# One queue in written order for the first cross attention, and a reordered step list in the last feed-forward block of a Perceiver kernel

## The chip, the core and the metric

The kernel is one program on one core of a Trainium2 chip. It is written in Tile: instructions are recorded tile by tile, the framework derives the semaphores, and outside of regions marked as manual a scheduler orders what each engine does. The metric is the device time of one execution in microseconds, as the median of the runs shown.

## The reference, cut to what matters

Twelve residual blocks follow each other on `x` of 2 x 256 tokens of 256 features (T = 512 columns, features on partitions), with a context of 2 x 4096 rows. Two of them are touched.

```python
# L0_xattn: 16 heads of 16, queries from layernorm(x), keys and values from the context
q = ln(x) @ Wq + bq;  k = ctx @ Wk + bk;  v = ctx @ Wv + bv
x = x + softmax(q k^T / 4 + mask) v
# L3_ffn: two layers of local attention (8 heads of 64, window 128, causal) and a gated MLP
q, k = l2norm(q) * qs, l2norm(k) * ks
q = q * cos * scale + rotate_half(q) * sin * scale        # k likewise, with 1 / scale
x = x + (softmax(8 q k^T + mask) v) @ wo
x = x + (a * gelu(g)) @ w2 + b2
```

All arithmetic is float32. The rest of the blocks, the key features of L3_xattn that are computed inside of L0_xattn among them, are not changed.

## The kernel before

**Cross attention.** `ContextAttention` works in 8 units, one per batch and group of four heads. A unit has 16 steps, and `attend` is a loop over all steps `g`. A step issues the first scores of its unit (`first_scores`, L1257: eight matmuls into four PSUM banks, whose maxima VectorE takes at L1265 and L1271), from step 18 on also the second scores of the unit before it (L1287), their exponentials on ScalarE (L1296) and the products with the values (L1308), and then the step's fills. A fill is a projection that a planner, `plan_with`, has placed by due times: a pair of key tiles (`project_keys`, L1167), half a value tile (`project_values`, L242 into `v_ps`) or key features for L3_xattn (`Focus.project`, L242 into `f_ps`). PE, VectorE and ScalarE follow the written order (`tc.manual_schedule`); GpSimd and SyncE, whose instructions are mostly DMA issues, are ordered by the scheduler.

**Keys.** A pair of key tiles needs two 512 KB loads of the context (`load_keys_ctx`, tiles `ctx_k`, one buffer each). In layer 0 the 2nd, 4th and 6th pair are loaded instead into six value tiles that are still free (`key_homes`, `xv` in the trace). After the matmuls ScalarE adds the bias (`k_dense`, L1177). Then `project_keys` issues the load for the next pair, two mask rows (L1185, 8 KB each) and eight copies of 16 rows (L1195, 32 KB each) that spread the dense keys to the head rows of `xa_k`. For the first six pairs the copies of the first tile go to ScalarE's DMA queue and those of the second to SyncE's; from the seventh on all go to SyncE's. Eight semaphores serve all of these DMAs in turn: the issue of a DMA waits until the DMA that used its semaphore last, eight earlier, has landed.

```python
queue = nc.scalar if self.spare and j < self.BY_ACT and i == 0 else nc.sync
for g in range(NG):
    at = i * HR + g * DH
    queue.dma_start(out=k[g * HP : g * HP + DH, :], in_=dense[at : at + DH, :])
```

**The last block.** `l3_ffn` makes queries and keys in four chunks of 128 features. `products` and `normalize` compute a chunk and its inverse norms (matmul with `same`, Ln and Exp on ScalarE at L2483 and L2484, the scaling on VectorE at L2485, four DMAs that swap halves), and `turn` applies the rotation (two multiplications at L2495 and L2496 for each of query and key, and a sum on GpSimd at L2497). `self_attention` then runs 16 items in pairs `m`. For each `m` it issues, in this order: `share` of the pair before (reciprocals on VectorE L460, the scaling of the probabilities on GpSimd L464), a hook `before`, the scores with their maxima (L419, L433) and exponentials (L445), a hook `along`, the weighing of the pair before that (L488, copied out by VectorE at L495), the transposes of the pair before (L475, copied out by VectorE at L480 and ScalarE at L478), and a hook `behind`, which `l3_ffn` does not use. Chunk 3 is normalized in `before(1)`, chunk 2 is turned in `along(1)`, chunk 3 in `along(3)` and `along(4)`.

Of the kernel before, what the change touches and what calls it, by code (L numbers as in the profile page):

```python
# [108 lines left out]
class Net:  # L109
# [51 lines left out]

    def load(self, *names, now=None):


        nc = self.nc
        t = self.weights.tile([P, 2048], F32, tag="w", name=f"w_{names[0]}")
        at, parts = 0, []
        for name in names:
            src = self.ins[name]
            n = int(np.prod(src.shape[1:]))  # L170
            letters = "abcde"[: len(src.shape) - 1]
            flat = src
            view = t[:, at : at + n]
            if len(letters) > 1:
                flat = src.rearrange(f"p {' '.join(letters)} -> p ({' '.join(letters)})")
                sizes = {c: s for c, s in zip(letters, src.shape[1:])}
                view = view.rearrange(f"p ({' '.join(letters)}) -> p {' '.join(letters)}", **sizes)
            issue = partial(nc.sync.dma_start, out=t[:, at : at + n], in_=flat)
            if now is None or len(parts) < now:
                issue()  # L180
            else:
                self.postponed.append(issue)
            parts.append(view)
            at += n
        assert at <= 2048, (names, at)
        return parts[0] if len(parts) == 1 else parts
# [331 lines left out]
    def context_attention(self, x, q_bias, k_bias, v_bias, wq, wk, values, layer, alive=None, block=None):  # L518

        tc = self.tc
        by_program = {mybir.EngineType.PE, mybir.EngineType.DVE, mybir.EngineType.Activation}  # L530
        to_values = lambda: tc.tile_pool(name="xa_v", bufs=1, reuse_waits="tile")
        with (
            tc.tile_pool(name="xa", bufs=1, reuse_waits="tile") as big,
            tc.tile_pool(name="xa_ctx", bufs=2, reuse_waits="tile") as cpool,
            to_values() if layer == 0 else nullcontext() as vpool,
        ):
            a = ContextAttention(self, layer, big, cpool, vpool, (wk, k_bias), v_bias)
            if layer == 0:
                for issue in self.postponed:
                    issue()  # L540
                a.load_keys_ctx()
                self.nc.sync.dma_start(out=self.vectors, in_=self.ins["vectors"])
                self.focus = Focus(self)
            a.wv, wo = values()
            if block is not None:
                with tc.manual_schedule(engines={mybir.EngineType.PE}), self.stage():
                    x = block(x, a.begin(3))
            with tc.manual_schedule(engines=by_program):
                return self.attend_to_context(a, x, q_bias, wq, wo, alive, nullcontext(vpool) if vpool else to_values())

    def attend_to_context(self, a, x, q_bias, wq, wo, alive, values):
        tc = self.tc
        with self.stage():
            norm = self.center(self.halves(x), load=a.layer > 0)
            if a.layer == 0:
                self.context_constants()
            if not a.begun:
                a.beginning = a.begin(2)
                run(a.beginning, 1)
            a.take_queries(norm, wq, q_bias, alive)  # L560
        with (
            self.banks(mm=4, sc=2, acc=0),
            values as vpool,
            tc.tile_pool(name="xa_p", bufs=1, reuse_waits="tile") as ppool,
            tc.tile_pool(name="focus", bufs=2, reuse_waits="tile") as fpool,
        ):
            return a.attend(vpool, ppool, fpool, x, wo)
# [237 lines left out]
class ContextAttention:  # L805
# [9 lines left out]
    VALUE_TILES = 11  # L815
    BY_ACT = 6
    SPARE = 3

    def __init__(self, net, layer, big, cpool, vpool, keys, v_bias):
        self.net, self.nc, self.layer, self.cpool = net, net.nc, layer, cpool  # L820
# [12 lines left out]
        if layer > 0:  # L833
            self.joined = Joined(net, big, lambda b, c: self.q[b * NC16 + c])
        self.spare = vpool is not None
        self.key_homes = {}
        if self.spare:
            self.vpool = vpool
            for n in range(self.SPARE):
                self.key_homes[2 * n + 1] = [self.new_values() for _ in range(2)]  # L840
        self.begun, self.beginning = 0, iter(())
# [248 lines left out]
    def attend(self, vpool, ppool, fpool, x, wo):  # L1090
# [4 lines left out]
        if self.layer == 0:  # L1095
            nc.gpsimd.memset(self.new[P // 2 :, ND - 1, S:], 0.0)
        for _ in range(4):
            self.load_values_ctx()
        focus.start(self.layer, fpool)
        fills = self.plan()  # L1100
        n = len(self.UNITS)

        rankings = {}
        for g in range((n + 1) * PER + LAG + 2):
            second = g - PER - LAG
            if 0 <= second < n * PER:
                self.scores(second // PER, second % PER)
            if g < n * PER:
                pair = self.first_scores(g // PER, g % PER)
            run(self.beginning)  # L1110
            if 1 <= g < n:
# [8 lines left out]
            for fill in fills.get(g, ()):  # L1120
                fill()
            for kc in self.rankings.get(g, ()):
                if kc not in rankings:
                    y, _, factor = focus.chunks[kc]
                    rankings[kc] = focus.sparsify(fpool, y, factor)
                run(rankings[kc], 1)
# [6 lines left out]
            for kc in self.weighings.get(g, ()):  # L1133
                run(focus.weighing[kc], 1)
        return self.new


    def load_keys_ctx(self):
        b, kc = next(self.key_loads, (None, None))
        if b is None:  # L1140
            return
        pair, homes = [], self.key_homes.pop(len(self.key_ctx), None)
        for i in range(2):
            if homes:
                flat = homes[i].rearrange("p k v -> p (k v)")[:, : ND * KC]
                ctx = flat.rearrange("p (d n) -> p d n", d=ND)
            else:
                ctx = self.cpool.tile([P, ND, KC], F32, name=f"ctx_k{i}", tag=f"ctx_k{i}", bufs=1)
            self.nc.sync.dma_start(out=ctx, in_=self.net.ins["ctxT"][b, kc + i])
            pair.append(ctx)  # L1150
        self.key_ctx.append(pair)

    def project_keys(self, j, first, n=1):
# [26 lines left out]
        tiles = [self.key_tiles[(2 * j + i) % self.KEY_TILES] for i in range(2)]  # L1180

        def write_mask(i):
            rows = tiles[i].rearrange("(g r) n -> g r n", r=HP)
            mask = net.key_masks[self.layer, b * NKC + kc + i]
            nc.sync.dma_start(out=rows[:, DH + 1], in_=mask.unsqueeze(0).to_broadcast([NG, KC]))  # L1185

        if not self.spare or j != 2 * self.SPARE - 1:
            self.load_keys_ctx()
        for i, k in enumerate(tiles):
            if j > 0:  # L1190
                write_mask(i)
            queue = nc.scalar if self.spare and j < self.BY_ACT and i == 0 else nc.sync
            for g in range(NG):
                at = i * HR + g * DH
                queue.dma_start(out=k[g * HP : g * HP + DH, :], in_=dense[at : at + DH, :])  # L1195
        if j == 0:
            for i in range(2):
                write_mask(i)

    def new_values(self):  # L1200
        return self.vpool.tile([P, KC // P, VW], F32, name="xv", tag="xv", bufs=self.VALUE_TILES)

# [9 lines left out]
    def project_values(self, b, kc, k2, first, n=1):  # L1212

        net, nc = self.net, self.nc
        if k2 == first == 0:
            v = self.new_values()
            nc.gpsimd.memset(v, 1.0)
            self.values[b, kc] = v
# [116 lines left out]
def l0_attn(net, x):  # L1335
    nc, tc = net.nc, net.tc
    wdq, wdkv, wuv = net.load("L0a_wdq", "L0a_wdkv", "L0a_wuv")
    wups = net.load("L0a_wuq", "L0a_wuk")
# [1065 lines left out]
def l3_ffn(net, x):  # L2404
# [8 lines left out]
    with tc.tile_pool(name="l3f", bufs=1, reuse_waits="tile") as big, tc.tile_pool(name="l3f_w", bufs=2, reuse_waits="tile") as work:  # L2413
# [24 lines left out]
        for layer in range(2):  # L2438
# [35 lines left out]

            def normalize(c, ps, sq):

                raw, swapped = (work.tile([P, 2, T], F32, tag=t, name=t) for t in ("raw", "swapped"))
                raws[c] = raw, swapped
                for i in range(2):
# [3 lines left out]
                    nc.scalar.activation(r, n2, AF.Ln, bias=tiny)  # L2483
                    nc.scalar.activation(r, r, AF.Exp, scale=-0.5)  # L2484
                    nc.vector.scalar_tensor_tensor(raw[:, i], r, 1e12, ps[i], ALU.min, ALU.mult)  # L2485
                HE = E // 2
# [13 lines left out]
            with tc.manual_schedule(engines=by_program):  # L2500
                made = {}
                for c in range(NCH - 1):
# [3 lines left out]
                    values(c)  # L2506
                    normalize(c, *made.pop(c))
                    if c == 1:
# [4 lines left out]
            def along(m):  # L2513
# [5 lines left out]
                if m == 1:  # L2519
                    turn(c - 1, alone=False)  # L2520
                if m in (3, 4):
                    turn(c, [m - 3], alone=False)

            def before(m):
                if m == 1:
                    normalize(NCH - 1, *made.pop(NCH - 1))

            def biases():
# [16 lines left out]
                along=along,  # L2545
                before=before,
            )
            moved = []
# [261 lines left out]
```

## Time and profile before

| | |
|---|---|
| median of 3 runs | 2142.94 us (2139.47 to 2145.37) |
| the profiled execution | 2143.32 us, its span 2141.3 us |
| busy share of the span | PE 96%, VectorE 65%, ScalarE 52%, GpSimd 21% |
| L0_xattn | from the start to about 714 us |
| attention of the two layers of L3_ffn | about 1943 to 1985 and 2050 to 2091 us |

PE, PEld, DVE, ACT and POOL are TensorE's matmuls, its weight loads, VectorE, ScalarE and GpSimd; SPq and ACTq are DMA issues on the queues of SyncE and ScalarE. All times are counted from the start of the span. In a row of the timeline the columns are start, duration of the group, engine, line, operation, output and inputs, shapes and count; in brackets stands how long the engine had been idle before, and what it waited for. Rows of a table by stretches give busy time of each engine in the stretch, and after the last engine the granted TensorE clock (1.00 is full speed), the DMA engines' busy share and GB/s.

### The profile page before, as it was taken

What the parts mean: (1) busy time and instruction counts of PE and PEld (TensorE: products, weight loads), DVE (VectorE), ACT (ScalarE), POOL (GpSimd) and SP (SyncE); (2) the same over time, 40 slices, a digit from 0 to 9 for tenths busy, and PEclk for the clock granted to TensorE, in tenths of its full rate; (3) what the DMA queues carried; (4) which work ended last, traced back from release to release, by engine and by line L of the source; (5) the groups of instructions that cost most, each with busy time, mean ns of one, the idle gap of its engine ahead of it and who ended that gap; (6) DMA issues with size and microseconds to landing.
All of it is one profiled execution on the core that took longest, in us unless ns stands there. A gap on an engine that the chain in (4) does not pass through costs nothing.

```text
span 2141.3 us, 54941 instructions
## 1 busy us (share of the span) xinstructions
PE 2052.3 (96%) x21271; PEld 1119.4 (52%) x21271; DVE 1396.5 (65%) x5226; ACT 1119.0 (52%) x2319; POOL 448.6 (21%) x699
## 2 busy tenths in 40 slices
PE   8899999999998989999999999999999998998989
PEld 3355555555554454555555555654448554554444
DVE  4788888878757669888888787453342274445353
ACT  2367666667756453676666677432122273336161
POOL 4122122221207412221221122000011040015050
PEclk9999999999999999999999999999999999999999
DMA  6433333323112234333333230311223011102120
GB/s 231 123 111 102 103 106 111 105 91 93 39 51 94 69 124 137 113 98 112 107 119 107 77 106 25 106 38 59 99 98 118 20 32 35 40 32 53 67 53 25
DMA packets 105171, 183.71 MB, mean 86 GB/s; under 512 B 17632, under 2 KB 68128, under 8 KB 104016
## 3 DMA queue, kind: packets, MB, share of 16 engines
q1 hardware_dynamic: 103840, 179.12, 26.6%
q8 instruction: 169, 2.77, 0.5%
q10 hardware_dynamic: 1072, 1.08, 0.2%
q14 instruction: 90, 0.74, 0.1%
HBM read 152.74 MB, written 0.59 MB: 72 GB/s over the span
## 4 chain that ended last, share of the span: by engine, by line
PE 56%; DVE 4%; ACT 4%; issue 1%; DMA 0%; POOL 0%; SPq 0%; DVEq 0%; ACTq 0%; POOLq 0%
PE attn_acc L1308 6%; PE s L1287 6%; PE s L1257 5%; PE proj L235 5%; PE expert L235 3%; PE s L235 3%; PE c_acc L2065 3%; PE v_ps L242 3%; PE k_ps L1167 2%; PE ffn_ps L235 2%; PE s L1732 2%; ACT p L445 1%; PE v_ps L235 1%; PE moe_acc L1940 1%; PE kc_sum L242 1%; PE kq_ps L235 1%
## 5 line engine op out<-in xcount | busy, mean ns | idle before, releaser
L1296 ACT ACTIVATE p<-s 128x512 f32<-128x512 f32 (+1 forms) x768 | 512.0, 740 | 149.0 <-PE s L1287 147.3
L1265 DVE TENSOR_REDUCE mx<-s 128x1 f32<-128x512 f32 x512 | 329.6, 685 | 163.0 <-PE s L1257 160.6
L1271 DVE TENSOR_REDUCE mx<-s 128x2 f32<-128x1024 f32 x256 | 311.3, 1216 | 0.0
L1287 PE MATMUL s<-xa_q,xa_k 32*128 32x256 f32 x4096 | 298.0, 400 | 0.7 <-DVE mx L1265 0.7
L1257 PE MATMUL s<-xa_k,xa_q 32*128 32x512 f32 x2048 | 287.3, 602 | 11.2 <-ACT xv L1226 7.6
L1323 POOL TENSOR_TENSOR a<-a,more 128x256 f32<-128x256 f32 x210 | 153.0, 729 | 678.4 <-ACT more L1322 676.0
L1308 PE MATMUL attn_acc<-p,xv 128*32 128x256 f32 x4096 | 276.3, 385 | 5.4 <-ACT p L1296 3.7
L1287 PEld LDWEIGHTS s<-xa_q,xa_k 32*128 32x128 f32 x4096 | 188.4, 184 | 110.7 <-issue 50.6
L1308 PEld LDWEIGHTS attn_acc<-p,xv 128*32 128x32 f32 x4096 | 111.6, 109 | 227.0 <-ACT p L1296 163.4
L732 DVE MATCH_REPLACE8 fy<-least,fy 128x16 f32<-128x16 f32 x1024 | 162.5, 174 | 0.0
L1257 PEld LDWEIGHTS s<-xa_k,xa_q 32*128 32x128 f32 x2048 | 111.0, 185 | 44.5 <-issue 16.1
L464 POOL TENSOR_SCALAR p<-p,r 128x128 f32<-128x128 f32 (+1 forms) x192 | 88.7, 481 | 83.9 <-DVE r L460 64.8
L726 DVE MAX8 least<-fy 128x8 f32<-128x16 f32 x1024 | 96.9, 171 | 1.1
L1322 ACT COPY more<-attn_acc 128x256 f32<-128x256 f32 x210 | 79.0, 376 | 12.7 <-PE attn_acc L1308 10.7
L732 DVE MATCH_VALUE_LOAD fy<-least,fy 128x8 f32 x1024 | 83.4, 81 | 0.5
L1226 ACT COPY xv<-v_ps 128x512 f32<-128x512 f32 (+1 forms) x78 | 39.7, 510 | 78.7 <-PE v_ps L242 76.1
L445 ACT ACTIVATE p<-p,top 128x256 f32<-128x256 f32 (+1 forms) x128 | 56.7, 444 | 38.5 <-DVE top L433 33.5
L1167 PE MATMUL k_ps<-ctx_k,w_L1x_wq 128*32 128x256 f32 (+1 forms) x768 | 66.1, 460 | 0.0
L242 PE MATMUL kc_sum<-f_tok,fy 128*32 128x129 f32 (+2 forms) x1536 | 65.3, 309 | 0.0
L242 PE MATMUL v_ps<-w_L1x_wv,ctx_v 128*32 128x256 f32 x1024 | 62.7, 380 | 0.0
L242 PE MATMUL v_ps<-w_L0x_wv,ctx_v 128*32 128x256 f32 x1024 | 62.7, 380 | 0.0
L242 PE MATMUL f_ps<-f_wk,f_ctx 128*32 128x256 f32 x1024 | 62.1, 380 | 0.0
(501 smaller groups left out, 3096.7 us busy)
## 6 DMA issues: line engine op xcount, KB each, us to landing
ctx_k<-in_ctxT SPq DMA_DIRECT2D x122, 512.0 KB
ctx_v<-in_ctxT SPq DMA_DIRECT2D x64, 256.0 KB
xa_k<-k_dense SPq DMA_DIRECT2D x488, 32.0 KB
f_ctx<-in_ctxT SPq DMA_DIRECT2D x32, 256.0 KB
f_tok<-in_ctx SPq DMA_DIRECT2D x16, 512.0 KB
swapped<-raw SPq DMA_DIRECT2D x64, 128.0 KB
ctxT<-in_ctxT SPq DMA_DIRECT2D x16, 512.0 KB
ctx_n<-in_ctx SPq DMA_DIRECT2D x16, 512.0 KB
```

Source lines behind the costliest of these rows:

```text
L235: self.nc.tensor.matmul(out, lhsT=lhsT, rhs=rhs, start=i == 0, stop=i == len(pairs) - 1)
L242: self.nc.tensor.matmul(out[cols], lhsT=lhsT[:, cols], rhs=rhs, start=i == 0, stop=i == len(pairs) - 1)
L726: nc.vector.max(least[:, i], w)
L732: nc.vector.match_replace(w, least[:, i], w, 0.0)
L1167: nc.tensor.matmul(ps[row : row + HP, :], lhsT=self.wk[:, d, col : col + HP], rhs=ctx[:, d, at], start=d == 0, stop=d == ND - 1,)
L1257: nc.tensor.matmul(banks[i], lhsT=self.q[u][rows, qt * P : (qt + 1) * P], rhs=k[rows, :], start=True, stop=True,)
L1265: nc.vector.tensor_reduce(mx[:, qt, i : i + 1, kc], sc, AX.X, ALU.max)
L1271: nc.vector.tensor_reduce(mx[:, n % 2, 2:, n // 2], pair, AX.X, ALU.max)
L1287: nc.tensor.matmul(banks[i][:, kk * S : (kk + 1) * S], lhsT=k[rows, at], rhs=self.q[u][rows, :], start=True, stop=True,)
L1296: nc.scalar.activation(p[:, i : i + sc.shape[1], :], sc, AF.Exp, scale=DH**-0.5)
L1308: nc.tensor.matmul(acc[i * HP : (i + 1) * HP], lhsT=v[:, 2 * k2 + kk, at : at + HP], rhs=ps[:, i, kk * S : (kk + 1) * S], start=kk == 0, s ...
L1323: nc.gpsimd.tensor_tensor(self.adding, self.adding, more, ALU.add)
```

## The change

L0_xattn: the spare homes are gone, so all keys are loaded into the two `ctx_k` tiles, and each load waits until the matmuls of the pair before are done. All row copies go to SyncE's queue. SyncE joins the engines that follow the written order from the first norm of L0_xattn to its end. The copies for the first pair are issued ahead of its masks, and one value tile is loaded at the start and three more in the first three steps, instead of four at the start. The second pair of keys is projected behind step 0's fill instead of ahead of it. The first weights of L0_attn are loaded behind step 32, with three one-column copies on ScalarE that claim their tile, where the scheduler used to place the load.

L3_ffn: `normalize` is split. In pair 1 the inverse norms of chunk 3 stay in `before`, the two scalings and the four DMAs move to `along`, behind the maxima; the turns of chunks 2 and 3 move from `along` to `behind`, behind the copies of the transposes; and four products of 128 x 512 in bf16 (`keep_busy`) are added in `along(2)`, ahead of the first weighing.

```diff
 # ContextAttention.project_keys
-            queue = nc.scalar if self.spare and j < self.BY_ACT and i == 0 else nc.sync
-            for g in range(NG):
-                queue.dma_start(out=k[g * HP : g * HP + DH, :], in_=dense[at : at + DH, :])
+        if self.layer == j == 0:
+            self.first_rows = lambda: (write_rows(0), write_rows(1), write_mask(0), write_mask(1), self.load_keys_ctx())
+            return
+        self.load_keys_ctx()
+        for i in range(2):
+            write_mask(i)
+            write_rows(i)          # four dma_start on nc.sync
 # context_attention
+            if layer == 0:
+                by_program.add(mybir.EngineType.SP)
 # attend
-        for _ in range(4):
+        for _ in range(4 if self.layer > 0 else 1):
             self.load_values_ctx()
...
+            if self.layer == 0 and g < 3:
+                self.load_values_ctx()
...
+            if self.layer == 0 and g == 2 * self.ORDERED:
+                net.first_of_l0_attn = net.load("L0a_wdq", "L0a_wdkv", "L0a_wuv", touch=True)
 # l3_ffn
             def along(m):
...
                 if m == 1:
-                    turn(c - 1, alone=False)
-                if m in (3, 4):
-                    turn(c, [m - 3], alone=False)
+                    normalize(c, *made.pop(c))
+                if m == 2:
+                    net.keep_busy(net.mm("busy"), 4)
             def before(m):
                 if m == 1:
-                    normalize(NCH - 1, *made.pop(NCH - 1))
+                    ps, sq = made[NCH - 1]
+                    made[NCH - 1] = ps, inverse_norms(sq)
+            def behind(m):
+                if m == 1:
+                    turn(NCH - 2, alone=False)
+                if m in (3, 4):
+                    turn(NCH - 1, [m - 3], alone=False)
```

More of the change, by code (lines that the diff above doesn't have):

```diff
@@ L160, in sm, with load @@
         return self.small.tile([P, *shape], dtype, tag=tag or f"sm{n}", name=name)
-    def load(self, *names, now=None):
+    def load(self, *names, now=None, touch=False):
         nc = self.nc
@@ L168, in load @@
         for name in names:
+            if touch:
+                nc.scalar.copy(t[:, at : at + 1], self.ones[:, 0:1])
             src = self.ins[name]
@@ L530, in context_attention @@
         by_program = {mybir.EngineType.PE, mybir.EngineType.DVE, mybir.EngineType.Activation}
[L531 to L537, printed above, removed]
+        with tc.tile_pool(name="xa", bufs=1, reuse_waits="tile") as big, tc.tile_pool(name="xa_ctx", bufs=2, reuse_waits="tile") as cpool:
+            a = ContextAttention(self, layer, big, cpool, (wk, k_bias), v_bias)
             if layer == 0:
@@ L540, in context_attention @@
                     issue()
-                a.load_keys_ctx()
                 self.nc.sync.dma_start(out=self.vectors, in_=self.ins["vectors"])
@@ L547, in context_attention, with attend_to_context @@
                     x = block(x, a.begin(3))
+            if layer == 0:
+                by_program.add(mybir.EngineType.SP)
             with tc.manual_schedule(engines=by_program):
-                return self.attend_to_context(a, x, q_bias, wq, wo, alive, nullcontext(vpool) if vpool else to_values())
-    def attend_to_context(self, a, x, q_bias, wq, wo, alive, values):
+                return self.attend_to_context(a, x, q_bias, wq, wo, alive)
+    def attend_to_context(self, a, x, q_bias, wq, wo, alive):
         tc = self.tc
@@ L562, in attend_to_context @@
             self.banks(mm=4, sc=2, acc=0),
-            values as vpool,
+            tc.tile_pool(name="xa_v", bufs=1, reuse_waits="tile") as vpool,
             tc.tile_pool(name="xa_p", bufs=1, reuse_waits="tile") as ppool,
@@ L815, with __init__ @@
     VALUE_TILES = 11
-    BY_ACT = 6
-    SPARE = 3
-    def __init__(self, net, layer, big, cpool, vpool, keys, v_bias):
+    ORDERED = 16
+    def __init__(self, net, layer, big, cpool, keys, v_bias):
         self.net, self.nc, self.layer, self.cpool = net, net.nc, layer, cpool
@@ L834, in __init__ @@
             self.joined = Joined(net, big, lambda b, c: self.q[b * NC16 + c])
[L835 to L840, printed above, removed]
         self.begun, self.beginning = 0, iter(())
@@ L1096, in attend @@
             nc.gpsimd.memset(self.new[P // 2 :, ND - 1, S:], 0.0)
-        for _ in range(4):
+        for _ in range(4 if self.layer > 0 else 1):
             self.load_values_ctx()
         focus.start(self.layer, fpool)
+        if self.layer == 0:
+            self.first_rows()
         fills = self.plan()
@@ L1103, in attend, with step @@
         rankings = {}
-        for g in range((n + 1) * PER + LAG + 2):
+        def step(g):
             second = g - PER - LAG
@@ L1109, in attend @@
                 pair = self.first_scores(g // PER, g % PER)
-            run(self.beginning)
+            if self.layer == 0 and g < 3:
+                self.load_values_ctx()
+            if self.layer > 0:
+                run(self.beginning)
             if 1 <= g < n:
@@ L1121, in attend @@
                 fill()
+            run(self.beginning)
             for kc in self.rankings.get(g, ()):
@@ L1134, in attend @@
                 run(focus.weighing[kc], 1)
+        for g in range((n + 1) * PER + LAG + 2):
+            step(g)
+            if self.layer == 0 and g == 2 * self.ORDERED:
+                net.first_of_l0_attn = net.load("L0a_wdq", "L0a_wdkv", "L0a_wuv", touch=True)
         return self.new
@@ L1141, in load_keys_ctx @@
             return
-        pair, homes = [], self.key_homes.pop(len(self.key_ctx), None)
+        pair = []
         for i in range(2):
[L1144 to L1148, printed above, removed]
+            ctx = self.cpool.tile([P, ND, KC], F32, name=f"ctx_k{i}", tag=f"ctx_k{i}", bufs=1)
             self.nc.sync.dma_start(out=ctx, in_=self.net.ins["ctxT"][b, kc + i])
@@ L1180, in project_keys, with write_rows @@
         tiles = [self.key_tiles[(2 * j + i) % self.KEY_TILES] for i in range(2)]
+        def write_rows(i):
+            for g in range(NG):
+                at = i * HR + g * DH
+                nc.sync.dma_start(out=tiles[i][g * HP : g * HP + DH, :], in_=dense[at : at + DH, :])
         def write_mask(i):
@@ L1185, in write_mask @@
             nc.sync.dma_start(out=rows[:, DH + 1], in_=mask.unsqueeze(0).to_broadcast([NG, KC]))
[L1187 to L1191, printed above, removed]
-            queue = nc.scalar if self.spare and j < self.BY_ACT and i == 0 else nc.sync
-            for g in range(NG):
[L1194 to L1201, printed above, removed]
+        if self.layer == j == 0:
[5 more added lines that the diff above has]
+            write_rows(i)
     def load_values_ctx(self):
@@ L1215, in project_values @@
         if k2 == first == 0:
-            v = self.new_values()
+            v = self.vpool.tile([P, KC // P, VW], F32, name="xv", tag="xv", bufs=self.VALUE_TILES)
             nc.gpsimd.memset(v, 1.0)
@@ L1336, in l0_attn @@
     nc, tc = net.nc, net.tc
-    wdq, wdkv, wuv = net.load("L0a_wdq", "L0a_wdkv", "L0a_wuv")
+    wdq, wdkv, wuv = net.first_of_l0_attn
     wups = net.load("L0a_wuq", "L0a_wuk")
@@ L2473, in values, with inverse_norms @@
                 nc.vector.tensor_copy(v[:, t, :], ps)
-            def normalize(c, ps, sq):
-                raw, swapped = (work.tile([P, 2, T], F32, tag=t, name=t) for t in ("raw", "swapped"))
-                raws[c] = raw, swapped
+            def inverse_norms(sq):
+                made = []
                 for i in range(2):
@@ L2484, in normalize @@
                     nc.scalar.activation(r, r, AF.Exp, scale=-0.5)
+                    made.append(r)
+                return made
+            def normalize(c, ps, rs):
+                raw, swapped = (work.tile([P, 2, T], F32, tag=t, name=t) for t in ("raw", "swapped"))
+                raws[c] = raw, swapped
+                for i, r in enumerate(rs):
                     nc.vector.scalar_tensor_tensor(raw[:, i], r, 1e12, ps[i], ALU.min, ALU.mult)
@@ L2506, in l3_ffn @@
                     values(c)
-                    normalize(c, *made.pop(c))
+                    ps, sq = made.pop(c)
+                    normalize(c, ps, inverse_norms(sq))
                     if c == 1:
@@ L2546, in l3_ffn @@
                 before=before,
+                behind=behind,
             )
```

## The prediction

> **What bounds the kernel now.** The page's busy shares come first: PE is busy for 96% of the span, the next engine for 65%. Whatever makes PE wait is lost; whatever happens elsewhere costs nothing until PE waits for it. So I read next a table by stretches over L0_xattn (PE, PEld, DVE, ACT, POOL busy, then granted clock, DMA share, GB/s):
>
> ```profile
> 24.20:52.80 28.60, 27.12 (x305) 10.02 (x304) 19.11 (x24) 6.60 (x16) 12.71 (x16) 1.00 0.64 200
> 52.80:60.20 7.40, 0.00 (x0) 0.00 (x0) 0.45 (x1) 1.59 (x3) 0.35 (x1) 0.73 0.67 186
> 60.20:69.20 9.00, 8.92 (x68) 2.73 (x68) 5.47 (x7) 1.20 (x3) 0.77 (x1) 0.65 0.43 125
> 100.00:714.00 614.00, 597.65 (x8110) 332.19 (x8100) 487.93 (x2060) 416.64 (x876) 157.12 (x227) 1.00 0.29 90
> ```
>
> In the second stretch PE does nothing at all, and in the third it works under a granted clock of 0.65. Later, the 614 us after 100 are nearly full, so only about 16 us are left for the change to gain there. The timeline of PE around the hole, and then ScalarE's:
>
> ```profile
> 50.74 1.93 PE L242 MATMUL v_ps<-w_L0x_wv,ctx_v 128*32 128x256 f32 x32
> 60.28 2.19 PE L1257 MATMUL s<-xa_k,xa_q 32*128 32x512 f32 x8 [7.60 <-ACT xv L1226]
> 62.40 3.64 PE L1167 MATMUL k_ps<-ctx_k,w_L0x_wk 128*32 128x512 f32 x16
> ```
> ```profile
> 46.90 0.69 ACT L1177 ACTIVATE k_dense<-k_ps,vectors 128x512 f32<-128x512 f32 x1 [1.72 <-PE k_ps L1167]
> 51.78 6.78 ACTq L1195 DMA_DIRECT2D xa_k<-k_dense  x4
> 58.61 1.15 ACT L696 ACTIVATE fy<-fy,eps 128x1024 f32<-128x1024 f32 x1 [11.02 <-DMA xa_k<-k_dense]
> 59.66 1.05 ACT L1226 COPY xv<-v_ps 128x512 f32<-128x512 f32 x2
> ```
>
> PE waits for a copy of values that ScalarE had no reason to delay: it stood 11.02 us in front of four DMA issues, each waiting for an earlier DMA to free its semaphore. ScalarE's table of waits has the same releaser four more times. The start has it too (the second row is PE's):
>
> ```profile
> 13.12 0.69 ACT L1177 ACTIVATE k_dense<-k_ps,vectors 128x512 f32<-128x512 f32 x1 [2.83 <-DMA vectors<-in_vectors]
> ...
> 16.44 0.26 ACT L335 ACTIVATE rstd<-var,eps 128x4 f32<-128x4 f32 x1 [2.63 <-DMA xa_k<-k_dense]
> ```
> ```profile
> 16.99 1.16 PE L235 MATMUL rstd_ps<-ident,rstd 128*128 128x128 f32 x8 [2.80 <-ACT rstd L336]
> ```
>
> **Row copies off ScalarE's queue, in unit 0 (gain).** A first step with nothing late takes 1.07 + 1.87 = 2.94 us (from 46.74 to 49.67). Step 1 starts at 29.56 and step 10 at 69.13, so nine steps take 39.57 us where 9 x 2.94 = 26.46 would do: 13.1 us lost. Of these 7.6 are the hole, about 2.8 the half clock behind it (2.19 for 1.14 and 3.64 for 1.93 above), 1.4 a wait of PE for `fy` L782 at 43.8, the rest stretched steps. All of it follows ScalarE's waits on `xa_k` DMAs, and the change leaves ScalarE no DMA: -13.1.
>
> **The start (gain).** One value load in place of four takes two loads of 1.3 us each from ahead of the vectors in the queue, so `k_dense` can run when `k_ps` ends (10.5) rather than at 13.12, and ScalarE issues nothing between. `rstd` then follows its `var` matmuls (end 12.4), and `rstd_ps` follows `q_ps`, which ends on PE at 14.2: about 14.0 for 16.99, so -3.0. The first copies, eight on one queue at 0.58 us, must land before the first scores, at about 21; two halves with the masks behind them end by about 20. No loss taken, up to 1 in the range. The second pair is projected behind step 0's fill, 2.7 us after the first scores; its loads land near 23.7, PE wants them at 24.8.
>
> **The prefetch that is dropped (cost).** Without spare homes the load for pair j+1 is issued when PE ends pair j. A pair that is alone in the queue lands in 5.5 us (first tile 3.5). Pair 2 is wanted 4.0 + 0.5 us after: +1.2. Pair 3 comes only three steps (8.8 us) later, with 15 issues in between (two loads, eight copies, two masks, three values at 0.58 = 8.7 us) before its own load has gone anywhere: +1.0. Pair 4: +0.2. Sum +2.4; bounds 0 (the waits of PE already in these steps cover it) and 6 (each also draws a slowed stretch).
>
> **SyncE in written order (cost).** This is the part whose price no row of before shows, since there the scheduler let independent loads pass. What one key block occupies:
>
> ```profile
> 154.18 0.81 SPq L1149 DMA_DIRECT2D ctx_k<-in_ctxT  x2
> 155.07 5.50 SPq L1195 DMA_DIRECT2D xa_k<-k_dense  x8
> 160.67 0.60 SPq L752 DMA_DIRECT2D f_ctx<-in_ctxT  x1
> ```
> ```profile
> 152.23 1.93 PE L1167 MATMUL k_ps<-ctx_k,w_L0x_wk 128*32 128x512 f32 x16
> ...
> 162.20 1.91 PE L242 MATMUL f_ps<-f_wk,f_ctx 128*32 128x256 f32 x32
> ```
>
> Loads, copies and masks hold the queue for about 7.3 us from the end of `k_ps` (154.2). In written order a load that stands behind them is issued at +7.3 and lands 3.1 us later, at +10.4. Where a block is followed two steps later by features, PE wants them 8.04 us after `k_ps` ends (154.16 to 162.20): +2.4. By the fill list that is so at steps 31 to 33 and 78 to 80; the other fourteen feature loads, and the values, have three steps of 4.67 us or more, 14 us against 10.4. Sum 2 x 2.4 = +4.8. Low bound 0 (the queue's copies wait less without others in between); high bound 10, four late blocks. Queued behind a waiting issue is every later load on SyncE; PE waits for those alone. Masks and copies have several steps.
>
> One rule of the Trainium skill speaks against the whole part: "DMA: Bandwidth & Descriptors", on issuing engines, says that spreading issues over engines saves only the sequencers' time, usually small beside the DMA. By it the move off ScalarE would be worth little, and the sum would lack its -13.1. The rows above measure the opposite here: four issues took 6.78 us on ScalarE and held it 11.02.
>
> **First weights of L0_attn, and touches.** Three one-column copies, near 0.2 us each (`rstd` of four columns takes 0.26 above), on an engine that is 68% busy from 100 to 714 us: nothing. The load itself moves from 54 us to step 32, away from the crowded stretch and long before its use: nothing.
>
> **L3_ffn.** What the change aims at is the wait of the first weighing, in each layer:
>
> ```profile
> 1956.99 1.64 POOL L2497 TENSOR_TENSOR qk<-raw,swapped 128x512 f32<-128x512 f32 x1 [4.08 <-DVE swapped L2496]
> 1959.25 1.27 POOL L2497 TENSOR_TENSOR qk<-raw,swapped 128x512 f32<-128x512 f32 x1 [0.63 <-DVE swapped L2496]
> 1960.50 1.63 POOL L464 TENSOR_SCALAR p<-p,r 128x128 f32<-128x128 f32 x4
> ```
> ```profile
> 1959.65 1.56 PE L488 MATMUL o<-pT,v 128*64 128x256 f32 x8 [3.20 <-DVE r L460]
> 1961.14 1.73 PE L475 MATMUL pT_ps<-ident,p 128*128 128x128 f32 x6
> ```
>
> VectorE copies the transposes out at 1959.1, behind four multiplications of a turn (3.55 us from 1955.6). With the turn behind that copy, the weighing can start near 1956.7. But the next work of PE, the transposes of pair 1, needs `p` from GpSimd (1960.50), which needs the reciprocals (1959.43 on VectorE) and comes after the turn's two sums. These do not get earlier: VectorE has the same multiplications before them. So the hole of 3.2 us before the weighing becomes one of 3.5 us behind it (57.6 to 61.1). The four dummy products (0.26 us each by the row of such a product at 1919.75: 1.03 for four) fill 1 us of waiting. Chunk 3's turns come 0.2 to 1.2 us ahead of later reciprocals. Taken as 0 per layer; bounds: -2.2 if the clock holds (1.56 to 0.88, 1.73 to 0.88, 1.64 to 0.93), with another -1 of idle, and +1 for the late reciprocals. The row: the granted clock falls to 0.62 at 1957 and 0.50 from 1959 to 1963 with the idle time.
>
> The skill's "TensorE: Matmul & The Clock Gate", Part 1, has the clock halved after an idle window of about 3.4 us; that would leave the moved hole just as costly, and the sum the same.
>
> **Sum.** -13.1 - 3.0 + 2.4 + 4.8 + 0 = -8.9. The profiled execution took 2143.32 us, 0.4 above the median of the runs: 2134.4, and 2134.0 on the median's scale. A measurement of this kernel can tell about 0.3%, 6.4 us, from no change: faster means below 2136.5, slower above 2149.4.
>
> **Rivals.**
> *A strict queue (slower).* One mechanism: in written order each late issue on SyncE delays every load behind it, at key blocks of later units too, 32 pairs in all. A late block costs 2.4 us. The gain of 16.1 less 2.4 at the prefetch is 13.7, used up by 6 late blocks; from 9 the kernel is measurably slower; with 11 it takes 2143 - 13.7 + 26.4 = 2156. For it: 0.58 us per issue and eight shared semaphores, so a copy that lands late holds the next. Against: 614 us at 90 GB/s and 29% DMA share, with steps of 4.67 us. Chance 0.10.
> *Stalls eat the gain (same).* 4 to 7 late blocks, or each late pair of the prefetch drawing a half clock as the hole did: 2137 to 2147. Chance 0.17.
> *The new waits are hidden.* Features and pairs arrive in time: only -13.1 - 3.0 and a rest, 2127 to 2130. For it: `f_ctx` alone lands in 3.1 us and copies can be issued faster when fewer wait. Chance 0.13.
> *L3_ffn gains as well.* The idle time in both layers goes and the clock stays: 3 to 6 us less than my sum, 2128 to 2131. Against: GpSimd's row at 1960.50. Chance 0.10.
> *My sum*: 0.50.
>
> **How the numbers follow.** The likeliest case gives 2134. From the two faster rivals the range takes all but their far end, and reaches to 2123 (the bounds 0 of the queue and the prefetch, and -2.2 in each layer); upward it takes the bounds 6 and 10, 2143. Left out are the slower rival and part of the same one. Faster: 0.13 + 0.10 + 0.50 = 0.73; same 0.17; slower 0.10.
>
> **What would show it.** Right: no wait of ScalarE on an `xa_k` DMA; first scores near 21 and no hole at 50 to 70, clock 1.00; `k_ps` waiting 1 us for `ctx_k` at pairs 2 and 3, `f_ps` waiting 2.4 for `f_ctx` at steps 33 and 80 and nowhere else; in L3_ffn an early weighing and then transposes that wait for GpSimd's `p`. Wrong: other waits of PE for `ctx_k`, `ctx_v`, `f_ctx` between 100 and 714, or a hole that only moved within unit 0; in L3_ffn, a stretch at clock 1.00 with no wait.

## The result, and the profile after

The changed kernel takes 2155.67 us (median of 6, 2151.78 to 2160.83) against 2144.15 us before: a ratio of 1.0055, 95% interval 1.0041 to 1.0069. It is slower by 11.5 us where 8.9 us less were forecast. The profiled execution of it took 2151.78 us (span 2149.7), the lowest of its runs, so its trace shows 8.4 us of the 11.5.

First the table by stretches, as before (PE, PEld, DVE, ACT, POOL busy, granted clock, DMA share, GB/s), of the changed kernel:

```profile
21.30:80.30 59.00, 53.75 (x602) 19.45 (x601) 42.55 (x82) 16.65 (x39) 17.69 (x23) 1.00 0.60 189
80.70:86.60 5.90, 0.04 (x2) 0.03 (x2) 3.49 (x16) 0.00 (x0) 0.00 (x0) 0.74 0.48 145
86.60:94.00 7.40, 7.40 (x64) 3.00 (x64) 3.48 (x16) 3.17 (x9) 0.00 (x0) 0.75 0.14 45
100.00:714.00 614.00, 593.16 (x8044) 328.50 (x8039) 480.85 (x2045) 412.08 (x864) 153.61 (x219) 0.99 0.29 92
```

The hole at 52.8 us is gone, and there is another at 80.7, with the half clock behind it as before. PE's table of waits up to 720 us says for what:

```profile
PE f_ps L244 <- DMA f_ctx<-in_ctxT: 10.7, 3, 5.9
...
PE k_ps L1165 <- DMA ctx_k<-in_ctxT: 5.2, 4, 2.3
```

No wait of PE for ScalarE in the first unit is left; ScalarE waits for an `xa_k` DMA once, 2.4 us. In their place stand seven waits for loads of the context. The timeline of PE has the places:

```profile
21.34 1.88 PE L1252 MATMUL s<-xa_k,xa_q 32*128 32x512 f32 x8
...
31.07 1.05 PE L1165 MATMUL k_ps<-ctx_k,w_L0x_wk 128*32 128x512 f32 x4 [0.27 <-DMA ctx_k<-in_ctxT]
33.00 1.91 PE L1165 MATMUL k_ps<-ctx_k,w_L0x_wk 128*32 128x512 f32 x12 [0.88 <-DMA ctx_k<-in_ctxT]
...
44.10 3.04 PE L1165 MATMUL k_ps<-ctx_k,w_L0x_wk 128*32 128x512 f32 x16 [2.25 <-DMA ctx_k<-in_ctxT]
...
68.56 1.93 PE L1165 MATMUL k_ps<-ctx_k,w_L0x_wk 128*32 128x512 f32 x16
...
86.60 1.94 PE L244 MATMUL f_ps<-f_wk,f_ctx 128*32 128x256 f32 x16 [5.86 <-DMA f_ctx<-in_ctxT]
...
163.95 1.93 PE L244 MATMUL f_ps<-f_wk,f_ctx 128*32 128x256 f32 x32 [2.41 <-DMA f_ctx<-in_ctxT]
...
369.95 3.45 PE L244 MATMUL f_ps<-f_wk,f_ctx 128*32 128x256 f32 x32 [2.44 <-DMA f_ctx<-in_ctxT]
```

And SyncE's queue ahead of the hole at 80.7:

```profile
70.05 1.96 SPq L1204 DMA_DIRECT2D ctx_v<-in_ctxT  x3
72.10 1.02 SPq L1147 DMA_DIRECT2D ctx_k<-in_ctxT  x2
73.22 0.55 SPq L1188 DMA_DIRECT2D xa_k<-key_masks  x1
73.85 3.73 SPq L1183 DMA_DIRECT2D xa_k<-k_dense  x4
77.68 0.52 SPq L1188 DMA_DIRECT2D xa_k<-key_masks  x1
79.48 2.98 SPq L1183 DMA_DIRECT2D xa_k<-k_dense  x4
82.57 0.61 SPq L1204 DMA_DIRECT2D ctx_v<-in_ctxT  x1
83.22 0.61 SPq L750 DMA_DIRECT2D f_ctx<-in_ctxT  x1
```

The feature load that PE wants at 80.7 (step 16; the expectations below call it step 18) is issued at 83.22. Its data and its buffer did not hold it: the projection that used the buffer last had ended by 37.84 us, and another kernel below (e6) issues the same load at 46.63. It stands in the queue behind the block of issues that starts at 70.05, and the queue has not run empty since 26.8 us. Row copies waiting for the semaphores of loads that had not landed are the largest part of the queue's waits. SyncE's table of waits from 20 to 90 us:

```profile
SPq L1183 <- DMA ctx_k<-in_ctxT: 9.1, 7, 2.6
```

**Where the 8.4 us are.** Each instruction of VectorE and ScalarE set against the same one of before gives how far the changed kernel is ahead or behind at that point:

| up to | behind by (us) | what came in |
|---|---|---|
| first scores | -2.8 | the start |
| end of the first unit, 75 us | -7.5 | unit 0: -13.1, and +8.5 at pairs 2 to 4 (+2.2, +3.4, +2.8, each from a step's length less 2.94) |
| 105 us | -1.1 | `f_ctx` at step 16: +6.4 |
| 200 us | +1.8 | `f_ctx` at step 33: +2.9 |
| 500 us | +5.8 | `f_ctx` at step 80: +4.1, of which 1.5 is half clock; -0.1 elsewhere |
| 700 us | +8.3 | +1.8 in a window of half clock (626.2 to 629.6 us) that before does not have, and +0.6 in waits at `scores` |
| 1930 us | +7.1 | windows of half clock at other places |
| 2110 us | +8.4 | L3_ffn, both layers: +1.3 |

### The profile page after: what moved, and what is told of

Its sections match the earlier page's. It is cut to its first block, busy times and chain, and to the rows that moved or that the text cites. A ratio compares the mean times of both kernels' runs of the same rounds, so it can differ in the third digit from the quotient of the medians.

```text
span 2149.7 us, 54921 instructions
## 1 busy us (share of the span) xinstructions
PE 2053.2 (96%) x21279; PEld 1117.8 (52%) x21279; DVE 1396.1 (65%) x5226; ACT 1119.3 (52%) x2322; POOL 447.3 (21%) x699
## 3 DMA queue, kind: packets, MB, share of 16 engines
q1 hardware_dynamic: 104608, 179.91, 26.8%
## 4 chain that ended last, share of the span: by engine, by line
PE 56%; DVE 5%; ACT 3%; issue 2%; DMA 1%; POOL 0%; SPq 0%; DVEq 0%; ACTq 0%; POOLq 0%
PE attn_acc L1303 6%; PE s L1282 6%; PE s L1252 5%; PE proj L237 5%; PE expert L237 3%; PE s L237 3%; PE c_acc L2060 3%; PE v_ps L244 3%; PE k_ps L1165 2%; PE ffn_ps L237 2%; PE s L1727 2%; PE v_ps L237 2%; ACT p L447 1%; PE moe_acc L1935 1%; PE qk_ps L237 1%
## 5 line engine op out<-in xcount | busy, mean ns | idle before, releaser
L1317 ACT COPY more<-attn_acc 128x256 f32<-128x256 f32 x210 | 79.0, 376 | 12.0 <-PE attn_acc L1303 10.2
L1165 PE MATMUL k_ps<-ctx_k,w_L0x_wk 128*32 128x256 f32 (+1 forms) x752 | 67.3, 457 | 5.3 <-DMA ctx_k<-in_ctxT 5.2
L477 PE MATMUL pT_ps<-ident,p 128*128 128x128 f32 x320 | 52.1, 291 | 14.1 <-POOL p L466 9.3
```

Source lines behind the costliest of these rows:

```text
L1165: nc.tensor.matmul(ps[row : row + HP, :], lhsT=self.wk[:, d, col : col + HP], rhs=ctx[:, d, at], start=d == 0, stop=d == ND - 1,)
```

## The experiments

Two theories stood against each other. **A**: the written order on SyncE costs the gain, because a load stands behind a key block that it does not need. **B**: dropping the prefetch (the spare homes) costs it, whatever the order. L3_ffn was the third suspect. Medians are set against the kernel before in the same set of runs (2143.9, 2144.4, 2144.2 and 2146.0 us for the four sets).

**e1_l3_only.** The kernel before with `l3_ffn` of the changed kernel.

> The kernel before with the L3_ffn part of the change alone. My step for it was 0 per layer: the hole of 3.2 us in front of the first weighing goes and one of about 3 us in front of the transposes of pair 1 comes, so 2144 within 2 us. If the L3_ffn part is what turned the forecast round, it is 8 us or more slower.

2147.52 us against 2143.93, ratio 1.0020 (1.0008 to 1.0031). The attention of its two layers lost only 1.0 us in its trace; the rest of the 3.6 shows in windows of half clock far from the edit (4.1 us between 1300 and 1930 us in the profiled run), so it is not settled how much of the 3.6 belongs to the edit. The time lies 1.5 us above the 2142 to 2146 that were expected. The part did not turn the forecast round.

**e2_l0_only.** The changed kernel with the `l3_ffn` of before.

> The change with the L3_ffn part undone. Theory A and B (the loss is in L0_xattn): within 2 us of the changed kernel, about 2154. If L3_ffn is to blame, close to the kernel before.

2151.49 us, ratio 1.0033 (1.0022 to 1.0044): 4.2 below the changed kernel where no more than 2 were expected, which puts a larger price on the L3_ffn part than the traces do. The larger part of the loss is in L0_xattn; its three waits for `f_ctx` are there with 10.5 us.

**e3_free_sync.** One statement out of the changed kernel:

```diff
-            if layer == 0:
-                by_program.add(mybir.EngineType.SP)
```

> The change without the written order for SyncE: the scheduler orders its queue again, everything else stays. Theory A (in written order feature loads stand behind a key block): the three waits for f_ctx, 5.9, 2.4 and 2.4 us idle and 3 us of half clock behind them, go, so 12 us less, about 2143. Theory B (without spare homes the pairs are loaded too late, whatever the order): no more than 3 us less, since the waits for ctx_k stay and the backlog that they cause as well.

2137.26 us, ratio 0.9965 (0.9952 to 0.9977): 18 us less than with the statement (14.5 by the spans of the two traces), and faster than before. In its trace PE waits for no `f_ctx`; the waits for `ctx_k` stay (3.9 us in five). Theory A expected 12, B no more than 3: A, and more of it than I had put on it. It shows too that the rest of the change is a gain.

**e4_rows_gpsimd.** The queue is kept in written order, and made shorter:

```diff
-                nc.sync.dma_start(...)
+                queue = nc.gpsimd if self.layer == i == 0 and j < 6 else nc.sync
+                queue.dma_start(...)
```

> The change with the row copies of the first tile of pairs 1 to 5 issued by GpSimd instead of SyncE, 20 copies of the 77 issues that SyncE makes between 20 and 85 us. Theory A in the form that SyncE is busy without a break from 26.8 to 85 us (too many issues in one queue): the backlog is 20 x 0.6 = 12 us shorter, the wait of 5.9 us at the second unit goes with its half clock (-6.4) and so do the waits for ctx_k at the 4th and 5th pair in part (-2), the two waits of 2.4 us later stay: about 2146. Theory B: the waits for ctx_k stay as they are, 1.2, 2.3 and 1.8 us, and the one of 5.9 us shrinks by what the queue is shorter.

2148.60 us, ratio 1.0022 (1.0007 to 1.0038), 7 less than the changed kernel. The edit moves the first pair's four copies too, 24 and not the 20 that the expectation names. The wait at step 16 went as expected, the two later ones stayed (1.9 us, and 2.7 us that the profile puts down to `fy`). At the pairs 3 and 4 PE did not wait any more, where theory B had them stay; but PE also came to them later, since GpSimd was late with its first copies, behind its memsets of the value tiles. PE stood 3.7 us at 40 us, at the step that needs the tile of these copies; the profile names no releaser there, so that it stood for them is inferred (PE, then GpSimd):

```profile
40.27 3.74 PE L1253 MATMUL s<-xa_k,xa_q 32*128 32x512 f32 x8 [3.68 <-issue]
```
```profile
27.56 6.02 POOL L1213 MEMSET xv<- 128x1148 f32 x6
33.54 1.99 POOL L1184 DMA_DIRECT2D xa_k<-k_dense  x4
```

**e5_homes, e7_homes_features, e10_late_homes.** The spare homes back in, in written order (e7 and e10 with the feature loads early as in e6):

```diff
+        if self.layer == 0:
+            self.key_homes = {2 * n + 1: [self.new_values() for _ in range(2)] for n in range(3)}
+            self.load_keys_ctx()          # e5, e7: ahead of the first rows; e10: behind them
```

> The change with the spare homes back (the 2nd, 4th and 6th pair go to six value tiles, and each load is issued one pair earlier); SyncE stays in written order with all row copies. Theory B (the dropped prefetch is what I mis-sized): the three waits for ctx_k, 1.2, 2.3 and 1.8 us, and 1.1 of half clock go, and since row copies no longer wait for the semaphores of loads that have not landed, the wait of 5.9 us at step 18 with 0.6 of half clock goes too: -12, about 2143; the two waits of 2.4 us at steps 33 and 80 stay. Theory A (written order alone): the ctx_k waits go, 6 us, and the 5.9 us stay, about 2149.

> Both repairs together: spare homes and feature loads one projection earlier, SyncE in written order. If the two causes are all that turned the gain round, no wait of PE for ctx_k or f_ctx is left, and the gains of the first unit and the start (13.1 and 3.0) stand alone beside L3_ffn: 2144 - 16 + 1 to 4, that is 2129 to 2132. If more than 2137, something else is lost in written order.

> As e7_homes_features, with the loads into the spare homes written behind the first rows and masks instead of ahead of them (e7 put them ahead, where they held the queue until the memory of the homes was free, and the first scores waited 9.8 us). Theory B with its price now measured on the changed kernel, 2.2 + 3.4 + 2.8 = 8.5 us for the pairs 2 to 4: with the homes and the early features both, PE waits for neither, so e6_features_early (2140.9) less 4 to 8 us, 2133 to 2137. Rival: the queue has no break from 27 to 85 us, so a prefetch only moves the lateness to the values (e5 waited 4.5 us for ctx_v); then no better than 2140.

e5: 2163.50 us, ratio 1.0088 (1.0055 to 1.0120); e7: 2150.68, 1.0027 (1.0011 to 1.0043); e10: 2144.70, 1.0005 (0.9996 to 1.0015). The first two miss every expectation by a fault of the experiment: their early load into a value tile waits until 21.8 us (e5) and 22.5 us (e7) for that memory, and in written order the first rows and masks wait behind it, so PE stands 10.2 and 9.8 us for `key_masks`. In e7 the waits for `ctx_k` and `f_ctx` are gone as expected, and PE waits 5.6 us for `ctx_v` instead. (The half clock that I put at pair 3 in e5's text was not there either: the granted clock was 1.00 at 44 us, and the 3.04 us are a split pair, see the last section.) e10 tests theory B cleanly, and its rival holds: the waits for the context of the keys shrink to 0.4 us, and the values are late instead. PE in e10:

```profile
67.86 3.64 PE L244 MATMUL v_ps<-w_L0x_wv,ctx_v 128*32 128x256 f32 x32 [5.97 <-DMA ctx_v<-in_ctxT]
```

Prefetched keys in a full queue push other loads back; 2144.7 is worse than without homes (e6). In the scheduler's order homes bought nothing either: e8 below has them and takes 2137.19 us, e9 has none and takes 2135.43, both with the old `l3_ffn` and all row copies on SyncE (they differ in smaller edits too). B is not the cause by itself.

**e6_features_early.** Each feature load is written where its buffer comes free, one projection earlier:

```diff
-            if t % 2 == 0:
+            if kc == t == 0:
                 self.load()
...
+            if t % 2 == 1:
+                self.load()
```

> The change with each feature load written one projection earlier, as soon as its buffer is free; nothing else differs from the changed kernel, written order for SyncE included. Theory A (it is the place of the loads in the written order that costs): all three waits for f_ctx go, 10.7 us and some 3 of half clock, about 2143. Theory B: the queue is late as a whole, the step 18 wait stays in good part, and only the 2 x 2.4 go, about 2150.

2140.85 us, ratio 0.9983 (0.9970 to 0.9996): 15 less than the changed kernel by the place of the feature loads alone (16 in L0_xattn; the edit also moves the 16 of the other cross attention, whose SyncE queue the scheduler orders). PE's waits up to 400 us, in e6, and the load for step 16 on SyncE:

```profile
PE k_ps L1167 <- DMA ctx_k<-in_ctxT: 4.2, 6, 1.8
```
```profile
46.63 0.60 SPq L750 DMA_DIRECT2D f_ctx<-in_ctxT  x1
```

`f_ctx` is not in the table. SyncE is as busy as in the changed kernel from 27 to 85 us, but what PE wants at step 16 was issued at 46.6 us.

**e8_before_rows_sync.** The kernel before with one constant changed, `BY_ACT = 6` to `0`.

> The kernel before with one constant changed (BY_ACT 6 to 0): all row copies on SyncE's queue, spare homes and the scheduler's order kept. It measures the term of -13.1 by itself: if ScalarE's wait in its DMA queue was the cause of the hole at 52.8 us, the hole and the half clock go and nothing new comes, 2144 - 13 + 0 to 3, about 2132. If the copies themselves are late on any queue, PE waits for SyncE's copies instead and it is 2140 or more.

2137.19 us, ratio 0.9967 (0.9955 to 0.9978): -7.0, between the two outcomes that the expectation names. The hole goes, and so do ScalarE's waits for `xa_k` but for one of 3.4 us, and the queue that takes the 24 copies is late with others, even in the scheduler's order. PE's steps 1 and 10 start at

```profile
30.53 1.14 PE L1257 MATMUL s<-xa_k,xa_q 32*128 32x512 f32 x8
...
57.72 1.14 PE L1257 MATMUL s<-xa_k,xa_q 32*128 32x512 f32 x8
```

so these nine steps take 27.19 us where the kernel before takes 39.57: -12.4, nearly the whole term. The start is 1.8 us earlier as well (first scores at 22.34 for 24.17). At 75 us of before's time the trace is 11.4 ahead, at 105 us only 5.7: a wait for values, half clock behind it and a wait of 1.4 us for VectorE take the difference back. PE's waits up to 100 us, in e8:

```profile
PE f_ps L242 <- DMA f_ctx<-in_ctxT: 2.6, 1, 2.6
PE v_ps L242 <- DMA ctx_v<-in_ctxT: 2.5, 1, 2.5
```

**e9_free_sync_old_l3, e12_more_dummies, e13_no_dummies.** All three are e3 with another `l3_ffn`: that of before; with 14 dummy products (`net.keep_busy(net.mm("busy"), 14)`); with none.

> As e3_free_sync (2137.3), with the L3_ffn part undone as well: a second reading of what that part costs, in another kernel. By the first reading, 2147.5 against 2143.9, it costs 3.6, so 2133.7; by the traces, which show 0.5 to 0.8 per layer, 1.3, so 2136.

> As e3_free_sync (2137.3), with 14 dummy products instead of 4 ahead of the first weighing in L3_ffn: 3.6 us of dummy work in place of 1.0, in front of a wait of 2.8 us for GpSimd's p. If the half clock behind that wait is what L3_ffn costs, it goes: 1 to 2 us less per layer, 2134 to 2136. If the wait has nothing to do with the clock, the weighing and with it the last steps come up to 1 us later and it is 2137 or more.

> As e3_free_sync (2137.3), without the 4 dummy products. By my reading they fill a wait and cost nothing: within 1 us; with fewer products the clock may fall earlier, up to +2.

e9: 2135.43 us, ratio 0.9958 (0.9944 to 0.9971); e12: 2135.15, 0.9958 (0.9943 to 0.9973); e13: 2136.74, 0.9964 (0.9952 to 0.9975). The medians lie within 2 us and their ranges overlap, so the stretch itself is read, as the change from 1930 to 2110 us against before: with 4 dummies +0.4 to +1.3 us (eight kernels), with none +1.3 (e13), with the old `l3_ffn` -0.4, -1.2 and -1.9 (e9, e2, e8), with 14 dummies -2.2 in each of the three kernels that have them. So before's own trace is the slowest of the four with the old `l3_ffn`, and 14 dummies beat that form by 0.3 to 2.2 us. PE in e3 and then in e12, layer 0:

```profile
1949.48 1.02 PE L252 MATMUL busy<-ident 128*128 128x512 bf16 x4 [1.27 <-ACT pT L480]
1950.43 0.88 PE L490 MATMUL o<-pT,v 128*64 128x256 f32 x8
1954.13 1.69 PE L477 MATMUL pT_ps<-ident,p 128*128 128x128 f32 x6 [2.83 <-POOL p L466]
1955.76 1.33 PE L421 MATMUL scores<-qk 64*128 64x128 f32 x8
```
```profile
1949.81 3.18 PE L252 MATMUL busy<-ident 128*128 128x512 bf16 x14 [1.26 <-ACT pT L480]
1952.92 0.88 PE L490 MATMUL o<-pT,v 128*64 128x256 f32 x8
1954.47 1.69 PE L477 MATMUL pT_ps<-ident,p 128*128 128x128 f32 x6 [0.68 <-POOL p L466]
1956.10 0.93 PE L421 MATMUL scores<-qk 64*128 64x128 f32 x8
```

The transposes start at the same distance from the dummies' start (4.65 and 4.66 us), so ten more dummies delay nothing; behind them `scores` takes 0.93 us and not 1.33. In e3 a window of half clock of 3.4 us begins behind this wait in each layer (at 1956.2 and 2062.0 us). In e15 and e16 there is none in the stretch; in e12 there are two, but later (1963.3 and 2069.2), and it gains the same 2.2 us. So the half clock directly behind the wait is there with four products and not with 14; that it explains all of the gain is not shown.

**e15_features_gpsimd, e16_free_gpsimd.** e6 and e3, each with 14 dummies, and the copies of e4 from pair 2 on (`2 <= j < 6`).

> As e6_features_early (2140.9), with the row copies of the first tile of pairs 2 to 5 issued by GpSimd, and 14 dummy products in L3_ffn (worth -2 in e12). Queue theory (too many issues in one queue): the waits for ctx_k at the pairs 3 and 4 go, as in e4, 2.0 + 1.3 and the 1.0 by which each split pair is longer; 2133 to 2135. Late-start theory (the loads are issued too late because their only two tiles come free too late): they stay, and it is 2138 to 2140.

> As e12_more_dummies (2135.2: SyncE in the scheduler's order, 14 dummy products), with the row copies of the first tile of pairs 2 to 5 issued by GpSimd. Queue theory: 3.3 us of waits for ctx_k and about 2 for split pairs go, 2130 to 2132. Late-start theory: 2135.

e15: 2135.38 us, ratio 0.9952 (0.9935 to 0.9968); e16: 2134.44, 0.9954 (0.9941 to 0.9967). Both beat the kernel before, and they, e9 and e12 cannot be told apart. In e15 the wait at pair 4 goes and that at pair 3 stays with 2.4 us; in e16 the waits for `ctx_k` stay as a whole (5.0 us in five). So the length of SyncE's queue makes one of the late pairs late in written order, and what is late in the scheduler's order is not explained by it. That the loads start late, because two tiles serve all pairs, fits e16, and e10 alone tried more homes, with the values late instead. This is left open.

## Why the prediction was wrong

**The start, -3.0.** The size was right, -2.8, first scores at 21.34, and so was the path, an earlier `k_dense`. But the two loads that no longer stand ahead of the vectors are not value loads, as the prediction has it: in the kernel before they are those into the first spare homes (3.29 us, the vectors at 4.26), and its first load of values is issued at 8.55, behind the vectors. The dropped homes gave this gain.

**Row copies off ScalarE, -13.1.** The mechanism was right, and the hole, its half clock and ScalarE's waits went, all but one of 2.4 us. The size was right where it was taken, -13.1 in the changed kernel and -12.4 in e8. As a term of a sum it was wrong, since it counted the copies out of one queue and nothing into the other: alone the move is worth -7.0, part of it the start (e8). The rule of the Trainium skill that I set against it ("DMA: Bandwidth & Descriptors", on issuing engines) has the sequencer's time saved by such a move, and calls it usually small; here it was not small, since the issues held ScalarE for 11.02 us, and the move was worth 7 us of 2144 in e8.

**The dropped prefetch, +2.4.** Mis-sized: +8.5, beyond its upper bound of 6. Pair 2 waited 1.15 us where 1.2 was worked out. The two terms that failed are the price of a late pair and the queue ahead of it. A pair whose first tile lands alone costs about 1.05 us more than its wait; that was in no row that I used (3.43 at pair 3 for a wait of 2.25, 2.80 at pair 4 for 1.77). And for pairs 3 and 4 I priced the queue at 0.58 us an issue, while between 20 and 90 us row copies waited 9.1 us in seven waits for the semaphores of `ctx_k` loads that had not landed.

**SyncE in written order, +4.8.** This is the step that turned the sign. The two waits that I named came where I put them and as long (2.41 and 2.44 us for 2.4), with 1.5 us of half clock behind the second. But the fourteen other feature loads were passed over with one sentence, "three steps of 4.67 us or more, 14 us against 10.4", and for the one at step 16 both numbers were wrong. From the end of the key block's `k_ps` (70.49 us, the row at 68.56) PE had three first-unit steps of 2.94 us and the first scores of the next, and wanted the features at 80.74, which is 10.3 us and not 14. And the load, written in the projection at 74.42, stood behind three value loads, the block's own issues and one more value load: it left at 83.22, 12.7 us after `k_ps` and not 7.3, and landed at 86.60, 16.1 after it and not 10.4. It alone cost 6.4 us. The three waits together are 13.4 us (6.4, 2.9 and 4.1) for 4.8, beyond the bound of 10. e3 and e6 show it from both sides: free order -18, the feature loads alone -15.

**The first weights of L0_attn** are issued at 161.13 us and PE waits for them nowhere, as taken.

**L3_ffn, 0.** The mechanism was right to the row: the weighing early, and a wait of 2.83 us for GpSimd's `p` behind it. PE in the changed kernel, layer 0:

```profile
1963.23 1.02 PE L252 MATMUL busy<-ident 128*128 128x512 bf16 x4 [1.27 <-ACT pT L480]
1964.18 0.88 PE L490 MATMUL o<-pT,v 128*64 128x256 f32 x8
1967.89 1.95 PE L477 MATMUL pT_ps<-ident,p 128*128 128x128 f32 x6 [2.83 <-POOL p L466]
```

It cost 1.3 us in the trace for a 0 with an upper bound of 1 per layer. The medians put more on it: 3.6 (e1 against before), 4.2 (the changed kernel against e2) and 1.8 (e3 against e9); which is right stays open. A gain needs what the change does not do: with 14 dummies e12 has -1.1 per layer against before's trace, half of the bound of -2.2. The second rule ("TensorE: Matmul & The Clock Gate", Part 1) says half clock after an idle window of about 3.4 us; here a window of 3.41 us at half clock came with the wait of 2.44 us at 369.95 and none with that of 2.41 us at 163.95, so these waits are where it can fall, not where it must.

**The rivals.** The strict queue ended on the right side and, by luck, near the right time (2156), with the wrong count: not eleven blocks at 2.4 us but three feature loads, one of them for 6.4, and three key pairs in the first unit. "L3_ffn gains as well" fell; "the new waits are hidden" fell. My chance of 0.10 for the strict queue came from later units (29% DMA share, steps of 4.67 us), where only two waits came; the queue was tight in the first unit, whose stretch showed a DMA share of 0.64.

**What the trace leaves open.** The medians differ by 11.5 us, the traces by 8.4. The runs of the changed kernel spread over 9 us; in the traces windows of half clock lie at other places from kernel to kernel in blocks that no edit touches. How the 3 us divide is not settled. The terms as measured, -2.8 - 13.1 + 8.5 + 13.4 + 1.3, make +7.3 of the 8.4.

## What to carry to other kernels

Before an engine's queue is put into written order, add up its issues and the waits on their shared semaphores over each stretch, and set that against the time that the stretch has: in the first unit, 77 issues (20 to 85 us) with their waits kept the queue from running empty from 27 to 85 us, and a load written behind others in it was then as late as the queue. In written order a load belongs where its buffer comes free, not where its user is; moving one load call in the code was worth 15 us here. A gain read from a hole counts the hole's end only up to the next thing that the moved work makes late.

## What the runs showed of the hardware

A pair of key tiles is projected by 16 matmuls that run four at a time, two for each tile. With both tiles there they take 1.9 us (56.54 us in e4: 1.92). When the first tile lands early, its first four run alone for 1.05 us and the other twelve still take 1.91 (31.07 and 33.00 above), so a half that is early shortens nothing and the split costs about 1.05 us beside the wait. At 44.10 us the same happens within one group: 3.04 us at a granted clock of 1.00.

Four bf16 products (1.02 us) in a wait of some 4 us left a window of half clock behind it in e3; with fourteen (3.18 us) there was none behind the same wait in e12, e15 and e16, and the work behind them came no later.
